# A macaron block with routed experts: one region of slots per expert for both sequences

## The chip, the cores and the metric

The kernel runs on one core of a Trainium2 chip. The metric is the device time of one execution in microseconds (us); lower is better. A run is compared by the median of several executions.

## The reference, cut to what matters

Two sequences of T = 2048 tokens with C = 256 features, all in float32. The same feed-forward part stands before and after a causal attention:

```python
x = x + 0.5 * ffn(layernorm(x))
x = x + attention(layernorm(x))      # one head of 128, causal
x = x + 0.5 * ffn(layernorm(x))

def ffn(x):
    xln = ln1(x)
    att_out = sigmoid(xln @ Wr) * (xln @ Wv) @ Wo
    rwkv_state = xln @ Ws
    x = x + att_out
    h = ln2(x)
    confidences = sigmoid of h against 3 vectors
    bids = confidences * capital_shares * sigmoid(h @ w_diff) + h @ W_aff
    winners = argmax(bids)                        # one of 3 experts per token
    experts 0, 1:  square(relu(h @ K_rwkv[e])) @ V_rwkv[e]      # 256 -> 1024 -> 256
    expert 2:      (h @ W1) * sigmoid(rwkv_state @ W2) @ W3     # 256 -> 256 -> 256
    return x + (the winner's output) * win_conf / (win_conf + 1e-6)
```

Each token needs one expert only. On the given inputs the reference routes, for experts 0, 1, 2: in the first feed-forward 416, 889, 743 tokens of the first sequence and 410, 910, 728 of the second; in the second one 379, 947, 722 and 415, 963, 670.

## The kernel before, in words

The kernel has two routed feed-forward stages and the attention between them.

**Routing.** `front` (L603) takes the tokens in groups of 512, four groups per sequence; `Group` (L346) holds their steps: a first norm, the gates `r` and `v` (L389, L397), the product with Wo (`mix`, L406), a second norm (`deviation`, `norm2`), the bids (`logits`, `choose`), each token's rank among its expert's tokens (`rank`, L503) and its slot (`slot`, L510). `move` (L528) then writes every token's row by an indirect DMA from GpSimd to a list in DRAM, `by_slot`. There is one such list for each sequence (L157), with a region for each expert and one blank block at its end. The order of the steps of different groups is written out by hand in `front`.

**Finish.** After a sequence's last group, `finish` (L554) counts the tokens per expert and computes `steer`: for every block of 256 slots its address in the list, for RWKV blocks the expert, and a flag that says whether more blocks are needed than are laid out. Slots behind the last token of an expert are filled with blank rows by three DMAs (L599), which later row loads wait for.

**Experts.** `experts` (L677) runs blocks of 256 rows (`BLK`). A block loads its rows from `by_slot` at an address that SP reads from `steer` (L754, L755), and an RWKV block also the expert's two weights of 1 MB each (L761, L763). TensorE transposes the rows (L689), the first product comes in pairs of 128 hidden columns (L704), with ReLU on ScalarE (L800) and the square on VectorE (L801); `back_to_rows` multiplies back (L718), VectorE scales and adds the residual (L728), and an indirect DMA writes each row to its token's place (L736): `x_mid` in the first stage, the output in the second. The token's number lies in the row itself. A number that is out of bounds is dropped.

Since the loop bounds are fixed, each sequence gets 3 transformer blocks (`GT_DONE`) and 6 RWKV blocks (`RW_DONE`), whether full or not: at most 3 x 256 tokens for expert 2 and six blocks for experts 0 and 1 together. Blocks beyond that stand in a branch (L842), which is taken if a flag is set. In the first stage the branch also fetches the tokens anew (`again`).

**Order of the work.** The first sequence is routed by itself (stage one) or beside the attention of the second sequence (stage two). Then `main`, the expert blocks, and `following`, the routing of the second sequence, are interleaved (L1042 to L1044, L1067 to L1069): in each turn one step of `main`, and two of `following`. An expert block has 6 or 8 steps. When the second sequence has its `steer`, the rest of `main` runs: the first sequence's other blocks, then those of the second. In the first stage, `ahead` (L1048) fetches the first sequence's new tokens for the attention and normalizes them beside the second sequence's blocks. A scheduler then orders the instructions of each engine by priority; only the first routing has a manual order. SP issues the loads in its own order, GpSimd the moves and the result scatters.

**Buffers.** Rows of blocks have three buffers (L753), weights two (L760, L762), results two. A row buffer is held until the scatter is done, since the scatter reads the token numbers from it.

Of the kernel before, what the change touches and what calls it, by code (L numbers as in the profile page):

```python
# [16 lines left out]
P = 128  # L17
# [20 lines left out]

BLK = 256
NI = BLK // P  # L40
RW_DONE = 6
GT_DONE = 3
# [31 lines left out]
def kernel(ctx: ExitStack, tc: tile.TileContext, a: dict, out: bass.AP):  # L74
# [8 lines left out]
    RW_MAX = T // BLK + 1  # L83
    GT_MAX = T // BLK
    REGION = T + BLK
    BLANK = E * REGION
    SLOTS = BLANK + BLK

# [25 lines left out]
    count = const.tile([P, RW_MAX], F32, name="count")  # L114
    starts = const.tile([P, RW_MAX], F32, name="starts")
    for n in range(RW_MAX):
        nc.gpsimd.memset(count[:, n : n + 1], float(n))
        nc.gpsimd.memset(starts[:, n : n + 1], float(n * BLK))


    ids = const.tile([P, B, ST], I32, name="ids")
    for b in range(B):
        nc.gpsimd.iota(ids[:, b, :], pattern=[[P, ST]], base=b * T, channel_multiplier=1)
    first = const.tile([P, E, TB], F32, name="first")
    for e in range(E):
        nc.gpsimd.memset(first[:, e, :], float(e * REGION))

    blank = const.tile([P, RW], F32, name="blank")
    nc.gpsimd.memset(blank, 0.0)
    nc.gpsimd.memset(blank[:, ID : ID + 1].bitcast(I32), NT)  # L130
# [9 lines left out]
    def fetch(work, seg, n, src, bufs, after=()):  # L140
# [4 lines left out]
        wait_for(nc.sync.dma_start(seg["x"][n], src).ins, after)  # L145
# [11 lines left out]
    by_slot = [dram.tile([SLOTS, RW], F32, name=f"by_slot{b}", tag=f"by_slot{b}") for b in range(B)]  # L157
    x_mid = [dram.tile([T, C], F32, name=f"x_mid{b}", tag=f"x_mid{b}") for b in range(B)]

    def slot_rows(b, slot, c=0):  # L160

        return by_slot[b][bass.ds(slot, BLK), c:].rearrange("(i p) d -> p i d", p=P)
# [182 lines left out]
    RW_AT, GT_AT, FILL_AT, MORE_AT, STEER = accumulate(RW_MAX, RW_MAX, GT_MAX, E, 1)  # L345

    class Group:
# [81 lines left out]
        def route(self, part):  # L429
# [14 lines left out]
            if part == 0:  # L444
                return
            self.by_col = self.work.tile([P, P], F32, name="by_col", bufs=2)
            nc.scalar.copy(self.by_col, self.ps_c)
            nc.scalar.copy(
                self.rows[:, :, ID].bitcast(I32), self.seg["ids"][:, self.n * TB : (self.n + 1) * TB]
# [30 lines left out]
        def choose(self):  # L480
            upto = self.seg["upto"]
            conf = self.conf[:, 0:E, :]
# [44 lines left out]
        def move(self):  # L527
            for t in range(TB):  # L528
# [3 lines left out]
                        out=by_slot[self.seg["b"]],  # L532
# [11 lines left out]
    def segment(b, numbers, bufs):  # L544

        upto = sort_pool.tile([P, E, ST + 1], F32, name="upto")
        nc.vector.memset(upto[:, :, 0], 0.0)
        groups.append(f"moves{b}_{len(groups)}")
        return {
            "b": b, "ids": numbers, "bufs": bufs, "rows": [], "x": [], "upto": upto, "moved": [],  # L550
# [516 lines left out]
    for _ in following:  # L1067
        next(main)
        next(following, None)  # L1069
# [43 lines left out]
```

## Time and profile before

| | us |
|---|---|
| median of 3 runs | 962.42 |
| these runs | 960.22 to 964.64 |
| the profiled execution, whole | 964.32 |
| its span in the profile | 962.6 |
| TensorE busy | 887.2 |
| VectorE busy | 458.9 |
| ScalarE busy | 320.5 |
| GpSimd busy | 191.5 |

The span is what the records of the profile cover; the whole time is 1.7 us longer. Busy times are those of one execution. In the lines of the profile, PE is TensorE's matmul and PEld its weight load, DVE is VectorE, ACT ScalarE, POOL GpSimd and SP the queue that issues most DMAs. A group of instructions has the line, engine, operation, output and inputs, the shape, how often it occurs, its busy time and the mean of one in ns, then the idle time ahead of it and what ended that. A line of the timeline has the start and the time from start to end in us, and in brackets the idle time just before.

### The profile page before, as it was taken

How to read it: one execution, taken by the hardware profiler on the slowest of the kernel's cores; microseconds unless marked ns; L12 is line 12 of the kernel's file. 1: busy time of each engine (PE TensorE's matmuls, PEld its weight loads, DVE VectorE, ACT ScalarE, POOL GpSimd, SP SyncE). 2: the span in 40 equal slices, each digit the busy share in tenths (PEclk: the TensorE clock that was granted, in tenths of full speed). 3: DMA queues.
4: the chain of work that ended last, by engine and by line, in shares of the span. 5: the costliest groups of instructions: out<-in, count | busy, mean ns of one | idle time of the engine just before them, and what ended most of it. 6: DMA issues, size and time to landing. Idle time of an engine off the chain costs nothing. (4 is left out here: it accounts for less than half of the span.)

```text
span 962.6 us, 12521 instructions
## 1 busy us (share of the span) xinstructions
PE 887.2 (92%) x4208; PEld 645.9 (67%) x4208; DVE 458.9 (48%) x1705; ACT 320.5 (33%) x692; POOL 191.5 (20%) x214
## 2 busy tenths in 40 slices
PE   5988889899989998888999999999989899999996
PEld 4555557688878886554455655555656688888885
DVE  2576765522234222367843578667575522222221
ACT  2343362312323220145442245264273212232220
POOL 2134333410132111000100102202232511121101
PEclk9988899999999999899999999999999999999998
DMA  9223535975449550200000001101525876438540
GB/s 291 103 101 142 184 124 192 329 231 195 132 145 345 190 173 20 88 0 1 1 0 1 1 1 67 67 0 67 199 109 186 300 230 211 134 131 293 196 161 22
DMA packets 67948, 129.06 MB, mean 134 GB/s; under 512 B 5020, under 2 KB 42781, under 8 KB 67872
## 3 DMA queue, kind: packets, MB, share of 16 engines
q1 hardware_dynamic: 57248, 92.92, 29.0%
q0 software_dynamic: 8576, 33.63, 9.2%
q10 hardware_dynamic: 2048, 1.58, 0.5%
q8 instruction: 37, 0.61, 0.3%
q14 instruction: 39, 0.32, 0.1%
HBM read 83.45 MB, written 45.71 MB: 134 GB/s over the span
## 5 line engine op out<-in xcount | busy, mean ns | idle before, releaser
L704 PE MATMUL ps_b<-cols,w_k 128*128 128x256 f32 x768 | 173.2, 384 | 0.9 <-DMA w_k<-in_K_rwkv_dram 0.5
L718 PE MATMUL acc<-w_e,hid 128*128 128x256 f32 x768 | 169.7, 379 | 0.0
L704 PEld LDWEIGHTS ps_b<-cols,w_k 128*128 128x128 f32 x768 | 148.0, 193 | 22.4 <-ACT cols L328 0.9
L718 PEld LDWEIGHTS acc<-w_e,hid 128*128 128x128 f32 x768 | 144.4, 190 | 18.8
L800 ACT ACTIVATE relu<-ps_b 128x512 f32<-128x512 f32 x96 | 57.2, 597 | 230.8 <-PE ps_b L704 230.4
L801 DVE TENSOR_TENSOR hid<-ps_b,relu 128x512 f32<-128x512 f32 x96 | 66.2, 691 | 108.7 <-ACT relu L800 106.6
L279 POOL TENSOR_TENSOR r<-ve,mhalf 128x4 f32<-128x4 f32 (+1 forms) x40 | 52.8, 1319 | 273.2 <-DVE ve L309 147.3
L728 DVE SCALAR_TENSOR_TENSOR res<-acc,rows_in 128x256 f32<-128x256 f32 x72 | 31.9, 479 | 145.8 <-PE acc L718 140.1
L531 POOL DMA_INDIRECT by_slot<-rows,slots x64 | 64.5, 1008 | 137.9 <-issue 62.1
L299 ACT ACTIVATE rows<-rows,shift,rstd 128x256 f32<-128x256 f32 x116 | 61.6, 593 | 78.0 <-DVE shift L295 72.3
L946 PE MATMUL ps_o<-p_tr,v 128*128 128x512 f32 (+3 forms) x160 | 74.5, 551 | 4.2 <-DVE p_tr L940 3.3
L736 POOL DMA_INDIRECT out_dram<-res,rows_in x36 | 35.3, 979 | 186.7 <-DVE res L728 154.1
L411 PE MATMUL acc<-w_o,gate_t 128*128 128x256 f32 x256 | 67.2, 412 | 2.6 <-DVE gate_t L400 2.5
L736 POOL DMA_INDIRECT x_mid<-res,rows_in x36 | 35.7, 991 | 166.9 <-DVE res L728 136.2
L893 PE MATMUL ps_s<-k_t,q_t 128*128 128x512 f32 (+3 forms) x160 | 65.2, 540 | 0.0
L909 ACT ACTIVATE prob<-ps_s,shift 128x512 f32<-128x512 f32 (+2 forms) x80 | 48.9, 620 | 48.7 <-DVE shift L906 44.5
L336 PE MATMUL ps_p<-y_t,w_r 128*128 128x512 f32 x128 | 63.3, 614 | 1.3 <-ACT y_t L384 1.3
L336 PE MATMUL ps_p<-y_t,w_v 128*128 128x512 f32 x128 | 61.5, 597 | 0.0
L411 PEld LDWEIGHTS acc<-w_o,gate_t 128*128 128x128 f32 x256 | 49.9, 204 | 15.2 <-DVE gate_t L400 5.3
L933 PEld LDWEIGHTS ps_pt<-ident,prob 128*128 128x128 f32 x272 | 32.8, 142 | 38.6 <-issue 14.3
L271 DVE BATCH_NORM_STATS2 stats<-rows 128x6 f32<-128x256 f32 x128 | 47.7, 413 | 13.4 <-DMA rows<-x_mid 8.7
L328 ACT ACTIVATE cols<-ps_bt,lnp 128x256 f32<-128x256 f32 x96 | 47.7, 561 | 19.0 <-PE ps_bt L689 19.0
(167 smaller groups left out, 1070.9 us busy)
## 6 DMA issues: line engine op xcount, KB each, us to landing
w_k<-in_K_rwkv_dram SPq DMA_DIRECT2D x24, 1024.0 KB, 6.3
w_e<-in_V_rwkv_dram SPq DMA_DIRECT2D x24, 1024.0 KB, 5.7
rows_in<-by_slot SPq DMA_DIRECT2D x24, 514.0 KB, 3.8
rows_in<-by_slot SPq DMA_DIRECT2D x12, 770.0 KB, 4.4
by_slot<-blank SPq DMA_DIRECT2D x6, 770.0 KB, 10.1
by_slot<-blank SPq DMA_DIRECT2D x8, 514.0 KB, 5.2
rows<-in_x_dram SPq DMA_DIRECT2D x8, 512.0 KB, 6.0
x_mid<-blank SPq DMA_DIRECT2D x1, 2048.0 KB, 12.4
```

The source lines that it names most:

```text
L279: nc.gpsimd.tensor_tensor(r0[:, 0:n, :], ve[:, 0:n, :], mhalf[:, 0:n, :], ALU.pow)
L299: nc.scalar.activation(dst[:, t, :], src[:, t, :], AF.Identity, bias=shift[:, t : t + 1], scale=r[:, t : t + 1])
L336: nc.tensor.matmul(ps, lhsT=w[:, k, m * P : (m + 1) * P], rhs=src_t[:, k, :], start=k == 0, stop=k == KC - 1)
L411: nc.tensor.matmul(acc[:, i, :], lhsT=self.gate_t[:, k, t * P : (t + 1) * P], rhs=w_o[:, k, :], start=k == 0, stop=k == KC - 1,)
L531: nc.gpsimd.indirect_dma_start(out=by_slot[self.seg["b"]], out_offset=bass.IndirectOffsetOnAxis(ap=self.slots[:, t : t + 1], axis=0), in_= ...
L704: nc.tensor.matmul(ps[:, j, :], lhsT=w[:, k, (m0 + j) * P : (m0 + j + 1) * P], rhs=cols[:, k, :], start=k == 0, stop=k == KC - 1,)
L718: nc.tensor.matmul(acc[:, i, :], lhsT=src[:, j, i * P : (i + 1) * P], rhs=w[:, j, :], start=j == 0, stop=j == n - 1,)
L736: ins = nc.gpsimd.indirect_dma_start(out=dests[b], out_offset=bass.IndirectOffsetOnAxis(ap=rows[:, i, ID : ID + 1].bitcast(I32), axis=0), ...
L800: nc.scalar.activation(relu, ps, AF.Relu)
L801: nc.vector.tensor_mul(self.mid[:, j : j + 2, :], ps, relu)
L893: nc.tensor.matmul(ps[:, :w], lhsT=seq["q_t"][:, qi * P : (qi + 1) * P], rhs=seq["k_t"][:, c * TG : c * TG + w], start=True, stop=True,)
L946: nc.tensor.matmul(ps_o[:, i0 * P :], lhsT=seq["v"][:, j, :], rhs=p_tr[:, i0 * P :], start=j == 0, stop=j == blocks - 1,)
```

## The change

There is one list for both sequences, with a region per expert that has a blank block at its head; the second sequence's slots follow those of the first (`choose` goes on from the first one's counts). The first `finish` lays out whole blocks of the first sequence only: 2 transformer and 4 RWKV. The second lays out the rest of both sequences: 4 transformer and 6 RWKV blocks of 256 rows, and then for each RWKV expert a half block of 128 rows. The last block of an expert starts early enough to end at its last token; its first rows, already done, are skipped by a number out of bounds (`skip`). Slots are no longer filled with blanks. Unused blocks read the blank block at address 0.

The token number is kept as a float, and `where` holds the integer address for the scatter. In the first stage, results of the first sequence's tokens must all come from the earlier blocks (`soon`), which the fetch for the attention waits for; `late` blocks drop such tokens (`early`), and the branch repairs it if there are any. The branch holds up to 12 transformer and 12 RWKV blocks in the second stage, more in the first. Each turn of the interleaving now takes three steps of `following`. `by_col` loses its second buffer.

```diff
-RW_DONE = 6
-GT_DONE = 3
+RW_WHOLE, RW_REST = 4, 6
+GT_WHOLE, GT_REST = 2, 4
...
-    RW_MAX = T // BLK + 1
-    GT_MAX = T // BLK
-    REGION = T + BLK
-    BLANK = E * REGION
-    SLOTS = BLANK + BLK
+    SQ = E - 1
+    POS = NT // BLK + SQ
+    REGION = BLK + NT
+    SLOTS = E * REGION
...
+    row_of = const.tile([P, NI], F32, name="row_of")
+    nc.vector.tensor_copy(row_of, ids[:, 0, 0:NI])
...
-    by_slot = [dram.tile([SLOTS, RW], F32, name=f"by_slot{b}", tag=f"by_slot{b}") for b in range(B)]
-    x_mid = [dram.tile([T, C], F32, name=f"x_mid{b}", tag=f"x_mid{b}") for b in range(B)]
-    def slot_rows(b, slot, c=0):
-        return by_slot[b][bass.ds(slot, BLK), c:].rearrange("(i p) d -> p i d", p=P)
+    by_slot = dram.tile([SLOTS, RW], F32, name="by_slot", tag="by_slot")
+    x_mid = dram.tile([NT, C], F32, name="x_mid", tag="x_mid")
+    def slot_rows(slot, n, c=0):
+        return by_slot[bass.ds(slot, n * P), c:].rearrange("(i p) d -> p i d", p=P)
...
-    RW_AT, GT_AT, FILL_AT, MORE_AT, STEER = accumulate(RW_MAX, RW_MAX, GT_MAX, E, 1)
+    RW_AT, GT_AT, HALF_AT, MORE_AT, STEER = accumulate(POS, POS, POS, SQ, 1)
...
-            self.by_col = self.work.tile([P, P], F32, name="by_col", bufs=2)
+            self.by_col = self.work.tile([P, P], F32, name="by_col")
...
+            if self.n == 0 and self.seg["prior"] is not None:
+                nc.vector.tensor_copy(upto[:, :, 0], self.seg["prior"]["upto"][:, :, ST])
...
     def finish(seg):
+        seg["skip"] = sort_pool.tile([P, STEER], F32, name="skip", bufs=1) if seg["prior"] is not None else None
+        (finish_whole if seg["prior"] is None else finish_rest)(seg, n_of, steer)
+        seg["steer"], seg["n_of"] = steer, n_of
+    def blocks_below(limits):
+        below = sort_pool.tile([P, E, POS], F32, name="below", bufs=1)
+        for e in range(E):
+            nc.vector.tensor_scalar(below[:, e, :], starts, limits[:, e : e + 1], None, ALU.is_lt)
+        number = sort_pool.tile([P, E], F32, name="number", bufs=1)
+        nc.vector.reduce_sum(number, below, axis=AX.X)
+        return number, below
+    def finish_whole(seg, n_of, steer):
+        limits = sort_pool.tile([P, E], F32, name="limits", bufs=1)
+        nc.vector.tensor_scalar_add(limits, n_of, float(1 - BLK))
+        whole, _ = blocks_below(limits)
+        valid = sort_pool.tile([P, POS], F32, name="valid", bufs=1)
...
+        second = sort_pool.tile([P, POS], F32, name="second", bufs=1)
+        nc.vector.tensor_scalar(second[:, 0:n], count[:, 0:n], whole[:, 0:1], None, ALU.is_ge)
+        nc.vector.tensor_copy(steer[:, 0:n], second[:, 0:n])
+        nc.vector.tensor_scalar(valid[:, 0:n], count[:, 0:n], shift[:, 1:2], None, ALU.is_lt)
+        nc.vector.scalar_tensor_tensor(
+            second[:, 0:n], second[:, 0:n], shift[:, 0:1], starts[:, 0:n], ALU.mult, ALU.add
+        )
+        nc.vector.scalar_tensor_tensor(
+            steer[:, RW_AT : RW_AT + n], second[:, 0:n], float(BLK), valid[:, 0:n], ALU.add, ALU.mult
+        )
...
+        done = seg["done"] = sort_pool.tile([P, E], F32, name="done")
+        nc.vector.tensor_scalar_min(done[:, 0:1], whole[:, 0:1], float(RW_WHOLE))
...
-        for e in range(E):
-            end = nc.sync.value_load(
-                steer[0:1, FILL_AT + e : FILL_AT + e + 1], min_val=e * REGION, max_val=e * REGION + T
-            )
-            c = YN if e == 2 else HN
-            moved(seg, nc.sync.dma_start(slot_rows(b, end, c), blank_rows(c)).ins)
...
+    def finish_rest(seg, n_of, steer):
+        done, n_first = seg["prior"]["done"], seg["prior"]["n_of"]
+        base = first[:, 0:SQ, 0]
+        limits = sort_pool.tile([P, E], F32, name="limits", bufs=1)
+        nc.vector.tensor_sub(limits, n_of, spare)
+        number, room = blocks_below(limits)
+        left = sort_pool.tile([P, E], F32, name="left", bufs=1)
+        nc.vector.tensor_sub(left, number, done)
+        last = sort_pool.tile([P, E], F32, name="last", bufs=1)
+        nc.vector.tensor_scalar_add(last, n_of, -float(BLK))
...
+        nc.vector.tensor_scalar(second, starts, at[:, 0:1], last[:, 2:3], ALU.add, ALU.min)
+        nc.vector.tensor_scalar(valid, count, left[:, 2:3], None, ALU.is_lt)
+        nc.vector.scalar_tensor_tensor(
+            steer[:, GT_AT : GT_AT + POS], second, float(SQ * REGION + BLK), valid, ALU.add, ALU.mult
+        )
+        more = sort_pool.tile([P, SQ], F32, name="more", bufs=1)
+        nc.vector.tensor_scalar(more, left[:, 0:SQ], -1.0, 0.0, ALU.add, ALU.max)
+        has = sort_pool.tile([P, E], F32, name="has", bufs=1)
+        nc.vector.tensor_sub(has[:, 0:SQ], left[:, 0:SQ], more)
...
+        nc.vector.scalar_tensor_tensor(
+            steer[:, RW_AT + SQ : RW_AT + POS], place, float(BLK), valid, ALU.add, ALU.mult
+        )
+        half = sort_pool.tile([P, 2, SQ], F32, name="half", bufs=1)
+        nc.vector.scalar_tensor_tensor(half[:, 0, :], number[:, 0:SQ], float(BLK), limits[:, 0:SQ], ALU.mult, ALU.min)
+        nc.vector.scalar_tensor_tensor(
+            skip[:, HALF_AT : HALF_AT + SQ], number[:, 0:SQ], float(BLK), limits[:, 0:SQ], ALU.mult, ALU.subtract
+        )
+        nc.vector.tensor_add(half[:, 0, :], half[:, 0, :], base)
+        nc.vector.scalar_tensor_tensor(half[:, 1, :], number[:, 0:SQ], float(BLK), n_of[:, 0:SQ], ALU.mult, ALU.is_lt)
+        nc.vector.tensor_mul(steer[:, HALF_AT : HALF_AT + SQ], half[:, 0, :], half[:, 1, :])
+        flags = sort_pool.tile([P, E + 2], F32, name="flags", bufs=1)
+        if seg["waited"]:
+            nc.vector.tensor_add(has, has, done)
+            nc.vector.scalar_tensor_tensor(flags[:, 0:E], has, float(BLK), n_first, ALU.mult, ALU.is_lt)
+        else:
...
+        nc.vector.tensor_scalar(flags[:, E : E + 1], at[:, 4:5], float(RW_REST - SQ), None, ALU.is_gt)
+        nc.vector.tensor_scalar(flags[:, E + 1 : E + 2], left[:, 2:3], float(GT_REST), None, ALU.is_gt)
+        nc.vector.reduce_max(at[:, 5:6], flags, axis=AX.X)
+        nc.vector.tensor_copy(steer[:, MORE_AT : MORE_AT + 1], at[:, 5:6])
...
+        def back_to_rows(src, w, n, rows, skip, group):
+            ni = rows.shape[1]
             acc = p_mm.tile([P, NI, C], F32, name="acc", tag="mm")
-            for i in range(NI):
+            for i in range(ni):
...
+            where = work.tile([P, NI], I32, name="where", bufs=2)
+            if skip is None:
+                nc.vector.tensor_copy(where[:, 0:ni], rows[:, :, ID])
+            else:
+                other = work.tile([P, NI], F32, name="other", bufs=2)
+                nc.vector.tensor_scalar(other[:, 0:ni], row_of[:, 0:ni], skip, float(NT), ALU.is_lt, ALU.mult)
+                if group is late and redo is not None:
+                    early = work.tile([P, NI], F32, name="early", bufs=2)
+                    nc.vector.tensor_scalar(early[:, 0:ni], rows[:, :, ID], float(T), float(NT), ALU.is_lt, ALU.mult)
+                    nc.vector.tensor_add(other[:, 0:ni], other[:, 0:ni], early[:, 0:ni])
+                nc.vector.tensor_add(where[:, 0:ni], other[:, 0:ni], rows[:, :, ID])
...
-                    out_offset=bass.IndirectOffsetOnAxis(ap=rows[:, i, ID : ID + 1].bitcast(I32), axis=0),
+                    out=dest,
+                    out_offset=bass.IndirectOffsetOnAxis(ap=where[:, i : i + 1], axis=0),
...
+                if group is not None:
+                    for one in sent.values():
+                        if one is group or one is soon:
+                            tc.declare_no_dep(
+                                ins, group=one["name"], reason="each token has a row of its own"
+                            )
+                    tc.add_to_no_dep_group(group["name"], ins)
+                    group["all"].append(ins)
...
-        def load_rows(b, at, c):
-            rows = work.tile([P, NI, RW], F32, name="rows_in", bufs=3)
-            slot = nc.sync.value_load(segs[b]["steer"][0:1, at : at + 1], min_val=0, max_val=BLANK)
-            wait_for(nc.sync.dma_start(rows[:, :, c:], slot_rows(b, slot, c)).ins, segs[b]["moved"])
+        def load_rows(b, at, n, c):
+            rows = work.tile([P, NI, RW], F32, name="rows_in", bufs=3)[:, 0:n, :]
+            slot = nc.sync.value_load(segs[b]["steer"][0:1, at : at + 1], min_val=0, max_val=SLOTS - BLK)
+            ins = nc.sync.dma_start(rows[:, :, c:], slot_rows(slot, n, c)).ins
+            if b == 0:
+                moves = segs[1]["moves"]
+                tc.declare_no_dep(ins, group=moves, reason="rows of the other segment's tokens")
+                tc.add_to_no_dep_group(moves, ins)
+            for seg in segs[: b + 1]:
+                wait_for(ins, seg["moved"])
             return rows
...
+                at, n, c = {
+                    "gt": (GT_AT, NI, YN), "rw": (RW_AT, NI, HN), "half": (HALF_AT, 1, HN)
+                }[self.kind]
+                self.at = at
+                self.rows = load_rows(self.b, at + self.n, n, c)
...
+                elif self.kind == "half":
+                    self.w = rw_weights(self.n)
...
+                n = self.cols.shape[2]
+                self.mid = work.tile([P, HC, BLK], F32, name="hid", bufs=2)[:, :, 0:n]
...
+                step = 2 * BLK // n
+                for j in range(0, HC, step):
+                    ps = several(self.w[0], j, self.cols)
...
-        todo = [("gt", n) for n in range(GT_DONE)] + [("rw", n) for n in range(RW_DONE)]
-        yield from pipelined([Block(b, *x) for b in range(B) for x in todo])
+        todo = [Block(0, "gt", n, soon) for n in range(GT_WHOLE)]
+        todo += [Block(0, "rw", n, soon) for n in range(RW_WHOLE)]
+        todo += [Block(1, "gt", 0, soon)] + [Block(1, "rw", n, soon) for n in range(SQ)]
+        todo += [Block(1, "gt", n, late) for n in range(1, GT_REST)]
+        todo += [Block(1, "rw", n, late) for n in range(SQ, RW_REST)]
+        todo += [Block(1, "half", n, late) for n in reversed(range(SQ))]
+        yield from pipelined(todo)
+        more = nc.values_load(segs[1]["steer"][0:1, MORE_AT : MORE_AT + 1], min_val=0, max_val=1)
         with tc.If(more > 0, preferred_fallthrough_block=False):
-            run(in_turn([Block(b, *x, branch=True) for b in range(B) for x in todo]))
+            again = redo is not None
+            todo = [("gt", n) for n in range(1 if again else GT_REST, NT // BLK)]
+            todo += [("rw", n) for n in range(SQ if again else RW_REST, POS)]
+            todo += [("half", n) for n in range(SQ) if again]
+            run(in_turn([Block(1, *x) for x in todo]))
             if redo is not None:
                 run(redo())
...
-            for b in range(B):
-                nc.sync.dma_start(slot_rows(b, BLANK), blank_rows())
+            for e in range(E):
+                nc.sync.dma_start(slot_rows(e * REGION, NI), blank_rows())
...
                 next(main)
-                next(following, None)
+                advance(following, 2)
...
-                fetch(front_pool, t0, n, token_tiles(x_mid[0], n), GB, s0["results"])
+                fetch(front_pool, t0, n, token_tiles(x_mid, n), GB, s0["results"], s1["moves_out"])
...
-    main = experts(expert_pool, [t0, t1], [out, out])
+    main = experts(expert_pool, [t0, t1], out)
...
         next(main)
-        next(following, None)
+        advance(following, 2)
```

## The prediction

> **What bounds the kernel now.** I read the page first: busy shares, the slices, then the costliest groups.
>
> ```profile
> PE 887.2 (92%) x4208; PEld 645.9 (67%) x4208; DVE 458.9 (48%) x1705; ACT 320.5 (33%) x692; POOL 191.5 (20%) x214
> PE   5988889899989998888999999999989899999996
> PEclk9988899999999999899999999999999999999998
> L704 PE MATMUL ps_b<-cols,w_k 128*128 128x256 f32 x768 | 173.2, 384 | 0.9 <-DMA w_k<-in_K_rwkv_dram 0.5
> L718 PE MATMUL acc<-w_e,hid 128*128 128x256 f32 x768 | 169.7, 379 | 0.0
> ```
>
> TensorE is busy in nearly every slice; no other engine reaches half. The two groups are the RWKV blocks: 768 records are 24 blocks of 32 (16 matmuls, two records each), so the overflow branch did not run. They hardly ever wait. Next, the timeline of TensorE in the last stage shows what one block costs.
>
> ```profile
> 388.09 1.95 PE L873 MATMUL ps_v<-wa_v,x_t 128*128 128x128 f32 x16
> 389.88 1.04 PE L322 MATMUL ps_t<-ident,rows 128*128 128x128 f32 x8
> ...
> 855.63 1.89 PE L704 MATMUL ps_b<-cols,w_s 128*128 128x256 f32 x8
> ...
> 861.93 1.89 PE L704 MATMUL ps_b<-cols,w_s 128*128 128x256 f32 x8
> ...
> 911.34 7.07 PE L704 MATMUL ps_b<-cols,w_k 128*128 128x256 f32 x32
> 918.25 0.60 PE L689 MATMUL ps_bt<-ident,rows_in 128*128 128x128 f32 x4
> 918.69 7.07 PE L718 MATMUL acc<-w_e,hid 128*128 128x256 f32 x32
> 925.60 7.07 PE L704 MATMUL ps_b<-cols,w_k 128*128 128x256 f32 x32
> ```
>
> From start to start an RWKV block takes 925.60 - 911.34 = 14.26 us: 6.91 + 0.44 + 6.91, so 0.216 us per record of 256 columns. A transformer block takes 6.30. The `ps_v` lines show 128 columns with new weights for every record: 1.79 us for 16, 0.112 each. Last, where the first sequence's blocks begin, TensorE does wait:
>
> ```profile
> 172.30 1.89 PE L704 MATMUL ps_b<-cols,w 128*128 128x256 f32 x8
> 176.31 1.99 PE L718 MATMUL acc<-w,gated 128*128 128x256 f32 x8 [2.12 <-DVE gated L793]
> 179.30 0.36 PE L504 MATMUL ps_rank<-wins,before 128*128 128x12 f32 x2 [1.00 <-DVE wins L493]
> 180.07 0.39 PE L505 MATMUL ps_rank<-upto,ones 128*128 128x12 f32 x2 [0.41 <-DVE upto L498]
> 182.04 8.71 PE L704 MATMUL ps_b<-cols,w_k 128*128 128x256 f32 x32 [0.22 <-ACT cols L328]
> ```
>
> The view by windows of the same place (busy time of PE, PEld, DVE, ACT, POOL, then TensorE's clock, DMA share, GB/s):
>
> ```profile
> 180.00:184.00 4.00, 3.70 (x17) 3.02 (x18) 2.95 (x28) 1.93 (x4) 2.72 (x4) 0.72 1.07 381
> ```
>
> Some 3.7 us of gaps, then a block at a lowered clock (0.72 here): 8.71 instead of 7.07. The same stands at 752 to 771 in the second stage.
>
> **What the Trainium skill says.** "TensorE: Matmul & The Clock Gate", section "LDWEIGHTS (loading the stationary operand)": a load takes the columns divided by 1.2 GHz, 107 ns for 128. The trace agrees in pace (0.112 us per record with a new load), though the record of one load lasts 192 ns; loads overlap. Same page, "What's actually happening": the clock falls to half after a quiet window of about 3.4 us. The trace agrees: the four-us windows before 180 have TensorE busy 2.19 and 2.36 us, then 0.72. "VectorE: DVE Perf Modes", "Rules for kernel authors": it is the number of operations that counts, not their semaphores. Here small operations last 0.15 to 0.23 us, and 24 of them at the first `finish` took 2.4 us (180.76 to 183.2), 0.10 each, because independent ones overlap.
>
> **The change, part by part.**
>
> *Blocks.* Per stage before: 2 x (6 RWKV + 3 transformer). After: 4 + 6 RWKV of 256 rows, 2 of 128 rows, 2 + 4 transformer. So each stage loses two RWKV blocks and gains two halves. A half: 32 records of 128 columns x 0.112 = 3.58; the second product has half the rows, 16 x 0.216 = 3.45; two transposes 0.22; sum 7.25 us. Saved: 2 x (14.26 - 7.25) = 14.0 per stage, 28.0 in all, on the engine that sets the end. Bounds: at 192 ns per record if the loads did not overlap, a half costs 2.6 more, 10.2 for four; it cannot be faster than its columns stream. I take 0.112. A half has two relu/square steps instead of four; ACT 0.60 and DVE 0.69 after 1.79 us of matmuls leave the second step ready 1.5 us on, and the product works 1.7 us on the first: no wait. Its weights are 2 MB per 7.25 us; `w_k` comes free half a block earlier, and the last `w_e` lands about 6 us (median 5.7) after the last full block, needed 10.8 us after it.
>
> *Does it all fit?* The reference's routing on its inputs gives, for experts 0, 1, 2 and both sequences, 826, 1799, 1471 tokens (stage one) and 794, 1910, 1392 (stage two); the first sequence has 416, 889, 743 and 379, 947, 722. That fills 1 + 3 whole RWKV and 2 transformer blocks at first, then 2 + 4 and 4, and both halves (58, 7 and 26, 118 rows). The flag stays 0.
>
> *Removed fills.* Twelve blank writes on SP with their register reads; row loads no longer wait for them. TensorE's first row transposes wait for DVE, not for these loads (124.02), so zero; one more blank write at the start lies under the first routing.
>
> *Routing of the second sequence*, now at three steps per expert step instead of two. From the compiled order, each group has 12 to 17 us of TensorE work from its `mix` to its rank; the chain needs 9 to 12 (mix end 34.0 to rank 43.2, 50.3 to 62.2). The order drops the transposes that stood behind `logits` (1.62 and 1.52 us), and puts six matmuls of the first RWKV block before the last rank wait. Gaps now about 5 us per stage; after, 0 to 1 between groups and some 2.2 at the end. I take -1.3 per stage, -2.6. Bounds: all gaps and the 1.7 us of slow clock gone, -6.8 per stage; or gaps and clock as where the first sequence is routed alone, +5.7 per stage (rival 1).
>
> *Longer `finish`* (`finish_rest`): 37 operations on DVE between the second and third square of an RWKV block, 4 to 5 us by the rate above. The product behind it has about 5 us of slack; I take +1.0 per stage, +2.0 (0 to 3 each). The first read of this `steer` stands on SP ahead of the third RWKV block's `w_k`, ten more ahead of its `w_e`; these are needed some 24 and 31 us later, zero.
>
> *Where to write.* 78 more operations of two columns on DVE, 0.16 each, 12.5 us; DVE is busy 6 of 25 us there, so zero. They wait for loaded rows with squares queued behind them; rows land 3.8 to 4.4 us after issue, a few us before. In return `rows_in` comes free before the scatter ends. `by_col` with one buffer is read by its transpose a whole group before it is written again: zero.
>
> *Three transformer blocks in a row beside the normalization* (stage one). Before, gaps 1.03 + 2.69 + 0.15 + 0.49 between 281 and 292. The row wait of 2.69 goes, but DVE has more statistics ahead of `gated`, which waits for rows that land 10 us into these blocks: +2.0. The single transformer block elsewhere adds 0.8 to stage two, for a wait like the 0.77 at 866. Bounds -3 to +5.
>
> *The end.* One scatter instead of two after the last matmul (starts 954.62 and 955.90): -1.3. Twenty more memsets on POOL at the start, 0.03 apart, lie in its 9.47 us wait.
>
> Sum: -28.0 - 2.6 + 2.0 + 2.8 - 1.3 = -27.1. The profiled execution took 964.3 (span 962.6 and 1.7 around it), so 937.2; it stood 1.9 above the median of 962.4, so 935.3. I say 935.
>
> **Rivals.**
> 1. The second routing starves. It would then behave like the first: some 2 us of gap per group and three half-clock stretches (a `mix` of 6.26 instead of 3.72). Three groups x (2 + 2.2) = 12.6 against 6.9 now: +5.7 per stage in place of -1.3, +14 in all: 949. For it: half of the expert work that covered routing is placed later; against: up to 17 us of work per group remain.
> 2. Narrow matmuls at the pace of their loads: +10, 945. The `ps_v` row speaks against.
> 3. The waits at the change of sequence vanish and the clock with them: 2 x -5.5 more and no DVE stall: 924 to 928.
> 4. Slower: the overflow branch runs. Its place is the end of stage two, its point expert 1 having over 7 x 256 + 128 = 1920 tokens (1910 counted), or its like elsewhere. Price: 12 transformer and 12 RWKV blocks, 12 x 6.3 + 12 x 14.26 = 247 us or more, unpipelined: 1182. Only if rounding moved ten tokens.
>
> **How the numbers follow.** Forecast 0.68, rival 1 0.12, rival 2 0.06, rival 3 0.08, rival 4 0.03, another slowdown that eats all of it 0.03. The range 926 to 947 has the unknown terms (clock, `finish`, narrow matmuls) and leaves out about 2 in 10. Half a per cent (4.8 us) is about what a measurement can tell. Faster by more: forecast and rivals 1 to 3, 0.94; same 0.02; slower 0.04.
>
> **What would show it.** Right: 20 full RWKV blocks of 14.26 us and four halves near 7.25, TensorE's busy sum down by about 28 us, one scatter at the end. Wrong: narrow records above 0.15 us apart; a lowered clock through 120 to 180 us; squares waiting for DVE at `finish` for over 3 us; any record after the end-of-stage branch that belongs to it.

## The result, and the profile after

The changed kernel took 990.96 us (median of 4 runs, 989.09 to 993.92), against 962.86 for the kernel before: 1.0297 times as long, with a 95% interval of 1.0261 to 1.0333. The forecast was 935 us, so it missed by 56 us and had the wrong sign. In the second of the three sets of runs below the kernel before took longer (988.5 us against 962.7 in the other two), so the runs of that set are held against each other.

The page of the changed kernel (busy time by engine, the slices, TensorE's product groups):

```profile
PE 874.0 (88%) x4136; PEld 630.3 (64%) x4136; DVE 464.1 (47%) x1831; ACT 315.1 (32%) x684; POOL 191.0 (19%) x232
PE   5988899988887997889999899999998997967995
L836 PE MATMUL acc<-w_e,hid 128*128 128x256 f32 x704 | 160.1, 382 | 14.5 <-DVE hid L948 14.5
L821 PE MATMUL ps_b<-cols,w_k 128*128 128x256 f32 (+1 forms) x768 | 159.1, 364 | 0.0
L836 PE MATMUL acc<-w,gated 128*128 128x256 f32 x96 | 33.7, 505 | 32.7 <-DVE gated L938 32.7
```

The work is smaller, as it was meant to be: 704 records of the second product are 20 blocks of 32 and 4 halves of 16, so the overflow branch did not run, and TensorE is busy 13 us less than before (874.0 against 887.2). But the span grew by 27.0 us. In the last two fields of a group, the idle time ahead of it, stands what was new: TensorE waits 14.5 us for `hid` and 32.7 us for `gated`, both made on VectorE. The kernel before waited 0.0 us for `hid`, and for `gated`:

```profile
L718 PE MATMUL acc<-w,gated 128*128 128x256 f32 x96 | 24.2, 388 | 6.2 <-DVE gated L793 6.2
```

Added up from TensorE's timeline, its marked gaps are 104.2 us against 66.0; of the 38 us more, 14.5 lie between 182 and 400 us and 22.2 after 775, in the expert blocks of the two stages and not in the routing.

One such wait in the last stage, in TensorE's timeline and then in VectorE's:

```profile
826.59 1.89 PE L821 MATMUL ps_b<-cols,w_s 128*128 128x256 f32 x8
828.31 1.89 PE L821 MATMUL ps_b<-cols,w 128*128 128x256 f32 x8
830.04 0.60 PE L805 MATMUL ps_bt<-ident,rows_in 128*128 128x128 f32 x4
836.07 3.78 PE L836 MATMUL acc<-w,gated 128*128 128x256 f32 x8 [5.43 <-DVE gated L938]
839.65 7.72 PE L821 MATMUL ps_b<-cols,w_k 128*128 128x256 f32 x32
```

```profile
826.79 0.88 DVE L859 SCALAR_TENSOR_TENSOR res<-acc,rows_in 128x256 f32<-128x256 f32 x2 [4.99 <-PE acc L836]
835.22 0.16 DVE L856 TENSOR_TENSOR where<-other,rows_in 128x2 int32<-128x2 f32 x1 [7.55 <-issue]
835.33 0.69 DVE L938 TENSOR_TENSOR gated<-ps_b,gt_sig 128x512 f32<-128x512 f32 x1
```

The inputs of `gated` are done at 830.2, but VectorE makes it at 835.33, because it stands idle for 7.55 us ahead of a `where` of 0.16 us that is next in its queue. `where` has nothing to do with this block's gate: it is the address of the *next* block's rows. Here the profile doesn't say what `where` waited for (the bracket has only "issue"). In an RWKV block of the first stage it does, VectorE and then GpSimd:

```profile
193.84 0.88 DVE L859 SCALAR_TENSOR_TENSOR res<-acc,rows_in 128x256 f32<-128x256 f32 x2 [4.55 <-PE acc L836]
195.77 0.69 DVE L948 TENSOR_TENSOR hid<-ps_b,relu 128x512 f32<-128x512 f32 x1 [1.05 <-ACT relu L947]
202.51 0.17 DVE L846 CAST where<-rows_in 128x2 int32<-128x2 f32 x1 [6.05 <-DMA x_mid<-res,where]
202.59 2.10 DVE L948 TENSOR_TENSOR hid<-ps_b,relu 128x512 f32<-128x512 f32 x3
```

```profile
194.60 0.99 POOL L867 DMA_INDIRECT x_mid<-res,where  x1 [6.07 <-DVE res L859]
195.90 1.00 POOL L867 DMA_INDIRECT x_mid<-res,where  x1 [0.30 <-issue]
```

The bracket names what ended the wait: not the rows, but the scatter of the block before, issued at 194.60 and 195.90. `where` has two buffers. Block B's `where` had long been written; this one is block C's, and it takes the buffer of block A, whose scatter, just begun, still reads its addresses there. Three of B's four squares stand behind it. The list of waits gives the sum over the kernel:

```profile
DVE where L856 <- DMA x_mid<-res,where: 47.3, 11, 5.5
DVE where L856 <- DMA out_dram<-res,where: 33.7, 9, 5.5
DVE where L856 <- issue: 30.7, 4, 8.1
DVE where L846 <- DMA x_mid<-res,where: 16.4, 4, 6.1
DVE where L846 <- DMA out_dram<-res,where: 15.6, 4, 5.1
```

That is 143.7 us on VectorE, of which 113.0 are put down to scatters by name. Much of it passes while TensorE still has other products to do; the rest shows as TensorE's 47.2 us of waits for `hid` and `gated`. A scatter looks short: its record on GpSimd is 0.98 us. The Trainium skill, "DMA: Bandwidth & Descriptors", section "Anatomy of one DMA — SWDGE (gpsimd) path", says that a DMA signals only when its last byte is confirmed in the target, with some 2 us fixed. The trace agrees in kind and gives more; the view of the tile `where` has, for all scatters that read it:

```profile
DMA to landing us min/median/max: 2.3/4.9/7.4
```

And a long wait is followed by slower records. In windows of four us (busy PE, PEld, DVE, ACT, POOL, then clock, DMA share, GB/s):

```profile
882.00:886.00 4.00, 1.02 (x9) 0.78 (x7) 0.00 (x0) 1.93 (x4) 0.00 (x0) 0.91 1.04 406
886.00:890.00 4.00, 1.97 (x5) 1.62 (x6) 0.94 (x3) 0.00 (x0) 0.00 (x0) 0.50 0.84 287
```

In the window with the end of a wait of 5.00 us TensorE's clock is at half (0.50), and the 8 records of the `gated` product behind it last 3.78 us instead of 1.99. This agrees with what the prediction quoted from "TensorE: Matmul & The Clock Gate", section "What's actually happening" (a quiet window of about 3.4 us). The edge is not sharp in this trace: a wait of 2.98 us leaves a product of 2.00 us (at 876.70), one of 2.90 us a product of 2.76 (at 290.31).

### The profile page after: what moved, and what is told of

Its sections match the earlier page's. It is cut to its first block, busy times and chain, and to the rows that moved or that the text cites. A ratio compares the mean times of both kernels' runs of the same rounds, so it can differ in the third digit from the quotient of the medians.

```text
span 989.6 us, 12348 instructions
## 1 busy us (share of the span) xinstructions
PE 874.0 (88%) x4136; PEld 630.3 (64%) x4136; DVE 464.1 (47%) x1831; ACT 315.1 (32%) x684; POOL 191.0 (19%) x232
## 5 line engine op out<-in xcount | busy, mean ns | idle before, releaser
L836 PE MATMUL acc<-w_e,hid 128*128 128x256 f32 x704 | 160.1, 382 | 14.5 <-DVE hid L948 14.5
L821 PE MATMUL ps_b<-cols,w_k 128*128 128x256 f32 (+1 forms) x768 | 159.1, 364 | 0.0
L836 PEld LDWEIGHTS acc<-w_e,hid 128*128 128x128 f32 x704 | 130.4, 190 | 37.1 <-DVE hid L948 20.2
L821 PEld LDWEIGHTS ps_b<-cols,w_k 128*128 128x128 f32 x768 | 137.5, 192 | 17.0
L947 ACT ACTIVATE relu<-ps_b 128x512 f32<-128x512 f32 x88 | 52.5, 596 | 253.0 <-PE ps_b L821 205.7
L948 DVE TENSOR_TENSOR hid<-ps_b,relu 128x512 f32<-128x512 f32 x88 | 59.0, 687 | 38.1 <-ACT relu L947 34.4
L424 PE MATMUL acc<-w_o,gate_t 128*128 128x256 f32 x256 | 71.8, 432 | 2.2 <-DVE gate_t L413 2.2
L867 POOL DMA_INDIRECT out_dram<-res,where x34 | 33.6, 988 | 180.2 <-DVE res L859 165.9
L867 POOL DMA_INDIRECT x_mid<-res,where x34 | 33.7, 991 | 156.7 <-DVE res L859 144.3
L836 PE MATMUL acc<-w,gated 128*128 128x256 f32 x96 | 33.7, 505 | 32.7 <-DVE gated L938 32.7
L1089 PEld LDWEIGHTS ps_pt<-ident,prob 128*128 128x128 f32 x272 | 32.8, 142 | 38.6 <-issue 14.5
```

The lines of the kernel that those rows point to most:

```text
L424: nc.tensor.matmul(acc[:, i, :], lhsT=self.gate_t[:, k, t * P : (t + 1) * P], rhs=w_o[:, k, :], start=k == 0, stop=k == KC - 1,)
L821: nc.tensor.matmul(ps[:, j, :], lhsT=w[:, k, (m0 + j) * P : (m0 + j + 1) * P], rhs=cols[:, k, :], start=k == 0, stop=k == KC - 1,)
L836: nc.tensor.matmul(acc[:, i, :], lhsT=src[:, j, i * P : (i + 1) * P], rhs=w[:, j, :], start=j == 0, stop=j == n - 1,)
L867: ins = nc.gpsimd.indirect_dma_start(out=dest, out_offset=bass.IndirectOffsetOnAxis(ap=where[:, i : i + 1], axis=0), in_=res[:, i, :], in_ ...
L947: nc.scalar.activation(relu, ps, AF.Relu)
L948: nc.vector.tensor_mul(self.mid[:, j : j + step, :], ps, relu)
```

## The experiments

**First set: is it this wait, and what in it?** The theory (A): VectorE stands at the write of `where`, and squares and gates queue behind. The rivals: VectorE waits for rows, or is held up by the number of small operations (B); routing or `finish` is at fault (C).

Four buffers in the changed kernel:

```diff
-            where = work.tile([P, NI], I32, name="where", bufs=2)
+            where = work.tile([P, NI], I32, name="where", bufs=4)
```

> The changed kernel with four buffers instead of two for the tile of target addresses, where; nothing else. Theory A (the vector engine stands at the write of where, because the write needs the buffer that the scatter just issued still reads, and the squares and gates of the block stand behind it): the 47 us of TensorE waits put down to hid (14.5) and gated (32.7) go but for some 5, and the slow products after them too (about 10 us): 937 to 945, faster than before. Theory B (the vector engine waits there for rows that are still on their way, or simply for the number of small operations): those do not depend on the buffers, so still 975 or more. Theory C (the routing with three steps a turn, or the longer finish, costs it): no change, 985 to 993.

Measured: 930.35 us, 0.9656 times the kernel before (0.9616 to 0.9696). That is below the 937 to 945 forecast. One number in one line is worth 60.6 us and turns the sign; B and C fall as the main cause. Profile against profile (span 989.6 to 927.5, 62.1 us): 43.3 are gaps of TensorE (104.2 to 60.9), 18.3 are records at a lower clock (busy 874.0 to 855.7), more than the 10 us that the forecast had put there.

```profile
L836 PE MATMUL acc<-w_e,hid 128*128 128x256 f32 x704 | 156.7, 380 | 0.7 <-DVE hid L948 0.4 <-DVE at L710 0.2
L836 PE MATMUL acc<-w,gated 128*128 128x256 f32 x96 | 25.8, 408 | 8.1 <-DVE gated L938 8.1
```

The wait for `hid` went from 14.5 to 0.7 us, for `gated` from 32.7 to 8.1, and the `gated` products themselves from 33.7 to 25.8.

The same wait on another engine: VectorE adds in float, GpSimd converts into `where`, still two buffers.

```diff
-                nc.vector.tensor_copy(where[:, 0:ni], rows[:, :, ID])
+                nc.gpsimd.tensor_copy(where[:, 0:ni], rows[:, :, ID])
...
-                other = work.tile([P, NI], F32, name="other", bufs=2)
+                other = work.tile([P, NI], F32, name="other", bufs=4)
...
-                nc.vector.tensor_add(where[:, 0:ni], other[:, 0:ni], rows[:, :, ID])
+                nc.vector.tensor_add(other[:, 0:ni], other[:, 0:ni], rows[:, :, ID])
+                nc.gpsimd.tensor_copy(where[:, 0:ni], other[:, 0:ni])
```

> The changed kernel with where still in two buffers, but converted on GpSimd; the vector engine only adds up the float in a tile of its own (other, four buffers). The same wait for the same scatter is there, on an engine that has only the next scatter behind it. Theory A (what costs is not the wait but the engine that stands in it): GpSimd waits about 5 us per block, TensorE's waits go as with four buffers, 937 to 946. Theory B (late rows, or small operations): the vector engine still reads the loaded rows early in its queue, so 975 or more. A third way: GpSimd is now late with the scatters and the moves, which would show as waits for by_slot or x_mid and a time between, 950 to 970.

Measured: 957.4 us (0.9944, 0.9925 to 0.9962): the third way, and not for the reason given there. GpSimd, then VectorE:

```profile
227.23 0.18 POOL L857 CAST where<-other 128x2 int32<-128x2 f32 x1 [6.29 <-DMA x_mid<-res,where]
```

```profile
219.79 0.69 DVE L949 TENSOR_TENSOR hid<-ps_b,relu 128x512 f32<-128x512 f32 x1 [1.48 <-ACT relu L948]
227.45 0.23 DVE L850 TENSOR_SCALAR other<-row_of,skip 128x2 f32<-128x2 f32 x1 [6.96 <-POOL where L857]
227.58 0.68 DVE L949 TENSOR_TENSOR hid<-ps_b,relu 128x512 f32<-128x512 f32 x1
```

The wait came back to VectorE through `other`. Its first operation reads only constants and `skip`, which are there once `finish` has run, so the scheduler puts it as far ahead as its buffers go, four blocks here, and then it waits for a conversion that waits for a scatter. Its four buffers did not help an operation whose inputs are always ready.

One part of the change alone, in the kernel before: a copy of the row numbers into `where`, with two buffers and with four.

```diff
+            where = work.tile([P, NI], I32, name="where", bufs=2)
+            nc.vector.tensor_copy(where, rows[:, :, ID].bitcast(I32))
...
-                    out_offset=bass.IndirectOffsetOnAxis(ap=rows[:, i, ID : ID + 1].bitcast(I32), axis=0),
+                    out_offset=bass.IndirectOffsetOnAxis(ap=where[:, i : i + 1], axis=0),
```

> The kernel before, with one part of the change alone: the row numbers are copied by the vector engine into a tile where of two buffers, which the scatter reads in place of the rows. Theory A: each block that follows another closely waits for the scatter of the one before; 24 RWKV blocks at about 0.8 and six to nine transformer blocks at about 5 plus 1.6 of slow clock behind each: 40 to 65 us more, 1000 to 1030. Theory B or C: 36 operations of 0.16 us beside 25 us of idle time each: 960 to 968.

> As the run before it, the kernel before with the copied row numbers, but with four buffers for where: the control. Theory A: the copies themselves cost nothing, 957 to 968, no difference that can be told from the kernel before. Theory B (the number of small operations, or the rows they read): the same as with two buffers.

Measured: 1021.03 us with two buffers (1.0601, 1.0556 to 1.0645), 970.73 with four (1.0067, 1.0042 to 1.0093). So 36 copies of 0.16 us cost 58 us in a kernel that had nothing else of the change. The last three transformer blocks of that run have the picture of the changed kernel:

```profile
893.21 2.44 PE L718 MATMUL acc<-w,gated 128*128 128x256 f32 x8 [2.76 <-DVE gated L795]
905.12 3.54 PE L718 MATMUL acc<-w,gated 128*128 128x256 f32 x8 [3.90 <-DVE gated L795]
918.24 3.78 PE L718 MATMUL acc<-w,gated 128*128 128x256 f32 x8 [5.70 <-DVE gated L795]
```

The control was to be neutral and is 8 us slower. With four buffers VectorE still waits 30.8 us for rows on their way, in 26 places, but these 8 us don't show B: TensorE never waits for `hid` in this run. Its largest new wait is one of 4.93 us for `gated` (1.03 there in the kernel before), with a product of 3.78 us behind it, where statistics of the tokens fetched for the attention stand ahead of the gate on VectorE and wait 3.91 us for their rows.

**Second set: buffers or place?** The forecasts in us were made from the times of the first set, so it is the comparisons within this set that count. In the compiled order the write of `where` stands one block ahead with two buffers, and two blocks ahead with three or with four, where the rows' own three buffers stop it.

```diff
-            where = work.tile([P, NI], I32, name="where", bufs=2)
+            where = work.tile([P, NI], I32, name="where", bufs=3)
```

> The changed kernel with three buffers for where instead of two. In the order of the compiled program the write of where stands exactly as far ahead as its buffers allow: with two buffers one block ahead of the block whose result is being made, with three buffers two blocks ahead (there the three buffers of the rows stop it), with four also two ahead. Theory A, sharpened (what counts is whether the buffer written was let go by the scatter just issued): with three buffers it is again the one just issued, so the stall stays, 975 to 1000. The plain reading (one buffer more takes the wait away): 928 to 938.

Measured: 946.40 us, where the kernel before took 988.51 (ratio 0.9571, 0.9541 to 0.9601). The sharpened theory missed: three buffers come within 4 us of the kernel further down in which the write is tied to its own product. Yet the wait it spoke of is there:

```profile
224.05 0.69 DVE L948 TENSOR_TENSOR hid<-ps_b,relu 128x512 f32<-128x512 f32 x1 [1.48 <-ACT relu L947]
225.78 0.69 DVE L948 TENSOR_TENSOR hid<-ps_b,relu 128x512 f32<-128x512 f32 x1 [1.03 <-ACT relu L947]
229.99 0.16 DVE L856 TENSOR_TENSOR where<-other,rows_in 128x2 int32<-128x2 f32 x1 [3.52 <-DMA x_mid<-res,where]
230.18 0.23 DVE L850 TENSOR_SCALAR other<-row_of,skip 128x2 f32<-128x2 f32 x1
230.32 1.28 DVE L948 TENSOR_TENSOR hid<-ps_b,relu 128x512 f32<-128x512 f32 x2
```

It is still the scatter just issued (55.3 us in all, against the 113.0 of the changed kernel). But the write now stands behind two or three of the running block's four squares, where in the changed kernel it stood behind one. A likely reason, not shown, is that the rows it reads, two blocks ahead, are loaded later. The scatter ends before the last squares are wanted. On this reading it is the place that counts: how many of the running block's squares stand behind the write while the scatter is in flight.

So the place alone was changed, with the two buffers kept:

```diff
-                    nc.tensor.matmul(
+                    mm = nc.tensor.matmul(
...
-                nc.vector.tensor_add(where[:, 0:ni], other[:, 0:ni], rows[:, :, ID])
+                to = nc.vector.tensor_add(where[:, 0:ni], other[:, 0:ni], rows[:, :, ID])
+            wait_for(to.ins, [mm.ins])
```

> The changed kernel with two buffers for where as it stands, but the write of where is made to follow the last matmul of its own block's product, so that it stands just ahead of the result (res) in the vector engine's queue. Same operations, same buffers. Theory A: the buffer then belongs to the block two before, whose scatter has ended, and the rows have landed too: TensorE's waits for hid and gated go, 924 to 933. If the number of buffers itself were what counts: 975 or more.

Measured: 942.52 us (0.9536, 0.9507 to 0.9564); 931.34 in the third set, where the kernel before took 962.70. With two buffers, the same operations and only another place in the queue the stall is gone:

```profile
209.45 0.69 DVE L949 TENSOR_TENSOR hid<-ps_b,relu 128x512 f32<-128x512 f32 x1 [1.04 <-ACT relu L948]
216.17 0.17 DVE L846 CAST where<-rows_in 128x2 int32<-128x2 f32 x1 [6.03 <-PE acc L836]
216.25 0.88 DVE L860 SCALAR_TENSOR_TENSOR res<-acc,rows_in 128x256 f32<-128x256 f32 x2
```

(This is VectorE in the third set's run.) VectorE now waits ahead of `where` for TensorE's own product, with all four squares made: a wait that holds nobody up.

The interleaving alone, undone on top of four buffers:

```diff
-                advance(following, 2)
+                advance(following, 1)
```

> Four buffers for where, and two steps of the second sequence's routing per turn as in the kernel before, in place of three. By the prediction three steps cost nothing to the routing's gaps and gain about 1.3 per stage, so this should be 930 to 936. If three steps starve the routing, two would be faster: 918 to 928. If the earlier end of the routing is worth much, slower: 937 to 945.

Measured: 958.50 us, 12.1 above three buffers and 16.0 above tied in the same set. This is the slower of the three forecasts, and beyond its 937 to 945: in this set three steps a turn are worth more than the 2.6 us that the prediction gave them. Four buffers with three steps were not run in this set. In the profile of two steps TensorE waits 7.5 and 9.5 us for `by_col` in the two second routings. But routing was slower in this set in any case: tied, TensorE waits 19.7 us in all for `by_col` and `wins`, and 13.2 us in the third set. So the size of this effect at the other sets' pace is not shown. Whether two steps would want back the second buffer that the change took from `by_col`, or the order of ScalarE's queue does it, was not tried.

The halves at full width, on top of four buffers (the 128 rows transposed and multiplied twice, only the first copy written):

```diff
-            ni = rows.shape[1]
+            ni = NI
...
-                        rows[:, i, at + c * P : at + (c + 1) * P],
+                        rows[:, min(i, rows.shape[1] - 1), at + c * P : at + (c + 1) * P],
...
-            for i in range(ni):
+            for i in range(NI):
```

> Four buffers for where, and the half blocks' matmuls widened to a whole block: the 128 rows are transposed twice and both copies multiplied, only the first is written. Prices the main term of the prediction (a half costs 7.25 against 14.26): four halves, 28 us more than with four buffers alone, 955 to 962. If narrow matmuls had no gain (bound by loading weights), less than 18 us more, under 949.

Measured: 972.92 us, above the 955 to 962 that was reckoned from the first set's times, but 26.5 above three buffers and 30.4 above tied in the same set, around the 28 forecast. Narrow matmuls keep their gain. The end of the kernel with four buffers shows it directly:

```profile
902.98 3.73 PE L821 MATMUL ps_b<-cols,w_k 128*128 128x128 f32 x32
906.55 0.38 PE L805 MATMUL ps_bt<-ident,rows_in 128*128 128x128 f32 x2
906.77 3.62 PE L836 MATMUL acc<-w_e,hid 128*128 128x256 f32 x16
910.22 3.73 PE L821 MATMUL ps_b<-cols,w_k 128*128 128x128 f32 x32
```

From start to start a half takes 910.22 - 902.98 = 7.24 us (7.25 forecast).

**Third set: the two cures side by side, and a better version.**

> Four buffers for where once more, on the chip that the three runs beside it use, since the kernel before took 26 us longer in the second set of runs than in the first. If the ratio to the kernel before holds across chips: 0.960 to 0.972. It is what the three others are held against.

> The write of where tied to its own product, two buffers, beside four buffers on one chip. If the writes no longer cost anything in either: within 4 us of each other. If the vector engine's 24 us of waiting for rows on their way, which is left with four buffers, still holds up squares: tied is faster by 3 to 8 us.

Measured: 929.73 (0.9660) and 931.34 us (0.9677), both intervals 0.0044 to either side. The ratio of four buffers holds, and the two cures are equal within their noise: VectorE's remaining 24 us of waiting for rows with four buffers cost nothing that can be measured here.

What was left in the first stage is a wait for `gated` beside the fetch of the new tokens (tied; TensorE, then VectorE):

```profile
282.97 3.78 PE L836 MATMUL acc<-w,gated 128*128 128x256 f32 x8 [6.28 <-DVE gated L939]
291.30 1.99 PE L836 MATMUL acc<-w,gated 128*128 128x256 f32 x8 [0.41 <-DVE gated L939]
```

```profile
276.50 0.43 DVE L284 BATCH_NORM_STATS2 stats<-rows 128x6 f32<-128x256 f32 x1 [3.02 <-DMA rows<-x_mid]
280.11 0.43 DVE L284 BATCH_NORM_STATS2 stats<-rows 128x6 f32<-128x256 f32 x1 [1.85 <-DMA rows<-x_mid]
282.24 0.68 DVE L939 TENSOR_TENSOR gated<-ps_b,gt_sig 128x512 f32<-128x512 f32 x1
```

The last kernel is tied too, and makes that fetch wait for the result of the third transformer block, so that its statistics don't queue ahead of the gates; it also issues twelve steps of the blocks before the fetch begins, and the two were not tried apart:

```diff
-                nc.vector.scalar_tensor_tensor(
+                made = nc.vector.scalar_tensor_tensor(
...
+                    group["last"].append(made.ins)
...
-                fetch(front_pool, t0, n, token_tiles(x_mid, n), GB, s0["results"], s1["moves_out"])
+                fetch(front_pool, t0, n, token_tiles(x_mid, n), GB, s0["results"] + blocks, s1["moves_out"])
...
+        advance(main, 12)
+        blocks = s1["last"][-1:]
```

> Tied, and the fetch of the first sequence's new tokens for the attention waits for the result of the third of the three transformer blocks in a row, so that its statistics don't stand ahead of their gates. Theory (the 6 to 7 us of TensorE waits for gated left in the first stage are statistics in the vector engine's queue that wait for fetched rows): 5 to 9 us faster than tied alone. If these waits are the blocks' own rows, or the attention then begins later for it: within 3 us, or slower.

Measured: 926.21 us (926.18 to 927.74 against 930.70 to 931.50 for tied), 5.1 faster and 0.9631 of the kernel before (0.9587 to 0.9675), the fastest version. Its TensorE timeline has one wait left in that stretch:

```profile
281.78 1.99 PE L837 MATMUL acc<-w,gated 128*128 128x256 f32 x8 [0.41 <-DVE gated L941]
```

Last, the control that should have been neutral, with the copy tied in the kernel before:

> The kernel before with the copied row numbers in two buffers, the copy tied to its own product. With two buffers and no tie it was 58 us slower than before, with four buffers 8 us. Theory A: position is all, the copies cost nothing: within 4 us of the kernel before. If the copies or the earlier release of the rows cost by themselves: 6 us or more slower, as with four buffers.

Measured: 966.56 us (1.0043, 1.0027 to 1.0059): 3.9 above, half of the 8 us with four buffers and a fifteenth of the 58 with two and no tie. Place explains nearly all. For the last 4 us the trace has a candidate, beside the fetch again: waits of 4.28 and 2.14 us for `gated` and products of 3.52 and 3.43 us instead of 1.99, where the kernel before had 4.4 us of gaps and no slow product. An estimate from these figures is 5 us. Taking it away in this kernel was not tried, so the cause of the 4 us stays open.

## Why the prediction was wrong, step by step

- **Where to write** (forecast: "zero") is the step that failed, by 60.6 us between medians. It priced 78 operations by their length, and asked of their waits only what they *read*: "They wait for loaded rows with squares queued behind them; rows land 3.8 to 4.4 us after issue, a few us before." It did not ask what they *write*. `where` has two buffers, each held until a scatter has landed, 4.9 us after issue. The prediction even counted as a gain that `rows_in` comes free before the scatter ends; the duty of being held until then had passed to `where`. The place it had right: it says itself that squares are queued behind these operations. So the zero rested on the rows landing in time; the wait that came was for a buffer.
- **Blocks** (-28.0): right. A half takes 7.24 us; widened, the four cost 26.5 to 30.4 more. Rival 2 falls.
- **Does it fit**: right, the branch did not run.
- **Routing** (-2.6): direction right, size too small. TensorE's gaps between 118 and 182 us and between 690 and 775 were 7.0 and 7.1; with four buffers they are 5.0 and 3.4, so -5.7. In the changed kernel that gain is not there (7.1 and 7.8). Rival 1 falls.
- **Finish** (+2.0): too much. In the changed kernel its operations take some 5.6 us (183.39 to 189, with two squares among them), a little over the 4 to 5 counted, but with four buffers TensorE waits only 0.16 and 0.44 us behind them. (The stretch of the kernel before from which the pace was taken has 22 operations and not 24, 0.11 us each; that changes little.)
- **Transformer blocks in a row** (+2.0 and +0.8): with four buffers 4.44 and 1.49 us of waits and one product of 3.43 instead of 1.99, against 4.4 us of gaps before, so +3.0 in the first stage; in the second 0.42 twice against 0.77, nothing.
- **The end** (-1.3): wrong sign. From the last `res` to the end of the span it was 962.6 - 953.86 = 8.7 us, and with four buffers 927.5 - 917.45 = 10.1. The single scatter starts as early as forecast and ends later; why was not tried.
- **The clock**: a reading was too quick. The prediction says that the trace agrees with a quiet window of about 3.4 us. Its own figures don't show one: before 180 no single gap is above 2.12 us and TensorE is busy for more than half of each window, yet the clock of the next window is 0.72. So several shorter gaps in a row went with a lowered clock too.

With four buffers the parts add up: TensorE's busy time -31.5, gaps -5.1, the end +1.3, together -35.3 for a span that fell by 35.1. The forecast of -27.1 would have been short of that by 8. The slower rival was the wrong one: the branch at 0.03, while "another slowdown that eats all of it" had 0.03 and no mechanism.

## What to carry to other kernels

For every operation that a change adds, ask four things: what it reads, which buffer it writes, who still reads that buffer and until when, and what stands behind it in its engine's queue in the compiled order. Here a tile that a DMA reads was held until the DMA had landed, not until its short record ended, and a tiny operation with ready inputs was placed as far ahead as its buffers allow. So tie such an operation to the work it belongs to, or give it so many buffers that the one it takes was let go a whole block ago.

## What the hardware showed that was not expected

- Gaps on TensorE cost almost half as much again in slower records: the 62.1 us between two and four buffers are 43.3 us of gaps and 18.3 us of slower records. One case stands above: after the wait of 5.43 us at 836.07 a product takes 3.78 us instead of 1.99 and the next 7.72 instead of 7.07, 2.4 us in all.
- The same kernel before took 962.7 us in two sets of runs and 988.5 in one; tied took 931.3 and 942.5. Its ratio to the kernel before was 0.9677 in one set and 0.9536 in the other, so a ratio of one set says little about a per cent in another. The record names the same chip for the first set and the second, so the chip does not explain it; what does stays open.
